# Attention followed by a GRU: an order of its own for the last batch of the attention

## The chip, the cores and the metric

The kernel runs on one core of a Trainium2 chip. The core has five engines that work side by side[...]: TensorE (PE in the profile; PEld is its weight load), VectorE (DVE), ScalarE (ACT), GpSimd (POOL) and SyncE (SP), which here issues DMAs. The metric is the device time of one execution in microseconds (us), as a median of several runs.

## The reference

The computation has two parts, each added to its input. `x` is (16, 256, 512): 16 batches of 256 time steps.

```python
# part 1: attention with 16 heads of 32 columns
scale, shift = split(cond @ W_emb + b_emb)
xn = rms_norm(x, g_norm) * (1 + scale) + shift
q, k, v = split(xn @ W_qkv)                # per head
q, k = rms_norm(q, g_q), rms_norm(k, g_k)
attn = softmax(q @ k.T * 32 ** -0.5)
o = attn @ v
x = x + o + o @ W_out
# part 2: a GRU over the 256 steps of the new x, started from cond
gi, gh = x_t @ W_ih + b_ih, h @ W_hh + b_hh
r, z = sigmoid(i_r + h_r), sigmoid(i_z + h_z)
n = tanh(i_n + r * h_n)
h = (1 - z) * n + z * h
out = x + hs
```

All arithmetic is in float32.

## The kernel before

The attention runs batch by batch, and in a batch by `NG` = 4 groups of `HG` = 4 heads. One group of one batch is a slot. `manual_schedule` makes the order in which the Python code issues instructions the order of each engine's queue (PE, DVE, ACT and POOL); semaphores are put in by the framework from the tiles that instructions read and write, so an instruction waits when it reaches the head of its queue, and all that is queued behind it waits too.

The work of a group, by function:

- `logits(b, g)` (L315): PE multiplies q and k of four heads into the PSUM banks lg0 to lg3, one bank a head.
- `maxima` (L332): DVE takes the negated row maxima, `neg`. `exps` (L340): ACT forms the exponentials, two instructions a head, into `attn`, with the row sums in `den`.
- `normalize` (L348, L351): DVE forms the reciprocals `rden`, POOL (or DVE) multiplies `attn` by them.
- `turn` (L224): PE transposes the four normalised heads, 32 small transposes into four banks. A bank holds one half of the rows of two heads. `put_turned` (L378) copies the four banks to `attnT` in SBUF, a string such as "vvva" naming the engine for each (v is DVE, a is ACT).
- `weigh` (L388): PE multiplies `attnT` with `v` into one bank. `put_weighed` (L399): ACT copies it to `oT`, which holds the attention's result, transposed, for all batches.

The slots are staggered: while the logits, maxima and exponentials of one group `w` are formed, the group before, `prev`, is transposed, copied and weighed. In batches 0 to 14 the slots (`slot0` to `slot3`) also hold the projections of the next batch, so PE has other work. Batch 15 has no next batch; its slots are `slot_last`:

```python
turn(prev, "AXYZ"); maxima(w, range(HG)); exps(w, range(HG))
put_turned(prev, "vvva")
normalize(w)            # in the last group heads 2 and 3 on DVE
weigh(prev, "A"); put_weighed(prev)
```

The main loop calls `logits(b, g)` ahead of it, and after the loop the last group is turned, copied ("vava") and weighed.

`attnT` has one buffer. PSUM has eight banks; in the attention they are the tags lg0 to lg3 (pool `ps_lg`) and A, X, Y, Z (pool `ps`). `work.close()` gives all of these back, and the GRU part opens three pools of its own: `ps_g` for the three gates (r, z, n), `ps_i` and `ps_o` with two buffers each for the input and output projections.

The GRU part works in stretches of `TI` = 16 time steps. `output_step` (L652, tile o) multiplies `wo` with `oT` (128 matmuls for a stretch, in four chunks m of 32), `put_output` (L685) adds each chunk to `xT`, the transposed x (DVE transposes it from `xin`, L667), and `input_step` (L652, tile gi) multiplies `wih` with `xT` (384 matmuls for a stretch). For the first stretch both run ahead of the recurrence; for the others they fill PE between the steps, four products a step (`FILL`). A step's own work is `state_part` (L714), the transposes L726 and the gates' arithmetic. `store_last` stores the last steps' results through a PSUM bank.

Of the kernel before, what the change touches and what calls it, by code (L numbers as in the profile page):

```python
# [19 lines left out]
def kernel(  # L20
# [57 lines left out]
    p1 = work.enter_context(tc.tile_pool(name="p1", bufs=1))  # L78
    p2 = work.enter_context(tc.tile_pool(name="p2", bufs=2))
    small = work.enter_context(tc.tile_pool(name="small", bufs=4))  # L80
    ps_lg = work.enter_context(tc.tile_pool(name="ps_lg", bufs=1, space=PSUM))
    ps = work.enter_context(tc.tile_pool(name="ps", bufs=1, space=PSUM))

# [136 lines left out]
    def turn_block(dst, src):  # L220

        for r in range(R):
            q = slice(QR * r, QR * r + QR)
            nc.tensor.transpose(dst[r], src[q], ident[q, q])  # L224
# [80 lines left out]
    def logits(b, g):  # L305

        w = Group()
        w.b, w.g = b, g
        w.lg = [
            ps_lg.tile([P, NT, T], F32, tag=f"lg{i}", name=f"lg_{b}_{g}_{i}") for i in range(HG)  # L310
        ]
        for n in range(NT):
            for i in range(HG):
                r = slice(i * DH, (i + 1) * DH)
                nc.tensor.matmul(  # L315
                    w.lg[i][:, n, :],
                    qT[r, g, n * P : (n + 1) * P],
                    kT[r, g, :],
                    start=True,
                    stop=True,  # L320
                )
        w.neg = small.tile([P, HG, NT], F32, tag="neg", name=f"neg_{b}_{g}")
# [23 lines left out]
    def normalize(w, heads=range(HG), engine=nc.gpsimd):  # L346
        r = slice(heads[0], heads[-1] + 1)
        nc.vector.reciprocal(w.rden[:, r, :], w.den[:, r, :])  # L348
        for i in heads:
            for n in range(NT):  # L350
# [2 lines left out]
                    ALU.mult, ALU.mult,  # L353
                )

    def turn(w, banks=("lg0", "lg1", "lg2", "lg3")):


        if w is None:
            return  # L360
        w.tp = [tile_ps(f"tpa_{w.b}_{w.g}_{i}", banks[i], (P, R, NT, NT, QR)) for i in range(HG)]
        for i in range(HG):
            for n in range(NT):
                for k in range(NT):
                    turn_block(
                        [w.tp[i // R * R + r][:, i % R, k, n, :] for r in range(R)],
                        w.attn[i][:, n, k * P : (k + 1) * P],
                    )
        w.attnT = p1.tile([P, HG, NT, T], F32, tag="attnT", name=f"attnT_{w.b}_{w.g}")

    def put_turned(w, engines):

        if w is None:
            return
        for i, e in enumerate(engines):
            h, r = i // R * R, i % R
            dst = w.attnT[:, h : h + R].rearrange("p h k (n r c) -> p h k n r c", n=NT, r=R)[:, :, :, :, r]
            (nc.scalar.copy if e == "a" else nc.vector.tensor_copy)(dst, w.tp[i])  # L378

    def weigh(w, bank):  # L380
        if w is None:
# [11 lines left out]
                    stop=(k == NT - 1),  # L393
                )

    def put_weighed(w):
        if w is None:
            return
        nc.scalar.copy(oT[:, w.g, :, w.b], w.o)  # L399

    class Stats:

# [108 lines left out]
            put_v(m, 1, st.v1)  # L511
        put_weighed(prev)

    def slot_last(g, w, prev):

        turn(prev, "AXYZ")
        maxima(w, range(HG))
        exps(w, range(HG))
        put_turned(prev, "vvva")
        if g < NG - 1:  # L520
            normalize(w)
        else:
            normalize(w, (0, 1))
            normalize(w, (2, 3), nc.vector)
        weigh(prev, "A")
        put_weighed(prev)

    E = mybir.EngineType
    ORDERED = {E.PE, E.DVE, E.Activation, E.Pool}
    with tc.manual_schedule(engines=ORDERED):  # L530

        nc.scalar.preload_act_table_set("natural_log_exp_and_others")
        st = Batch()
        norm_first(0)
        batches[0].rs.first()
        norm_apply(0, batches[0].rs.second())
        load_x(2)
# [42 lines left out]
        for b in range(B):  # L580
            for g in range(NG):
                w = logits(b, g)
                if b + 1 < B:
                    (slot0, slot1, slot2, slot3)[g](b, w, prev, st)
                else:
                    slot_last(g, w, prev)
                prev = w
        turn(prev)
        put_turned(prev, "vava")
        weigh(prev, "X")  # L590
        put_weighed(prev)

# [25 lines left out]


    gru = ctx.enter_context(tc.tile_pool(name="gru", bufs=2))
    ps_g = ctx.enter_context(tc.tile_pool(name="ps_g", bufs=1, space=PSUM))
    ps_i = ctx.enter_context(tc.tile_pool(name="ps_i", bufs=2, space=PSUM))
    ps_o = ctx.enter_context(tc.tile_pool(name="ps_o", bufs=2, space=PSUM))


    bhn_rows = gru.tile([P, P], F32, name="bhn_rows", bufs=1)
# [4 lines left out]


    gates = []
    for name in ("r", "z", "n"):
        gt = ps_g.tile([P, P], F32, tag=f"g{name}", name=f"g{name}")
        nc.vector.memset(gt, 0.0)
        gates.append(gt)

    TI = 16
    NI = T // TI
    NM = 3 * KC
    FILL = (KC + NM) * KC // TI
# [221 lines left out]
```

## Time and profile before

| | |
|---|---|
| Median of 3 runs | 1809.34 us (1808.86 to 1810.82) |
| The profiled execution | 1810.63 us, its span 1808.8 us |
| Granted TensorE clock, mean of the span | 0.994 |
| PE busy in the span | 1736.3 us (96%) |
| DVE, ACT and POOL busy | 1131.9, 819.8 and 314.4 us |
| Last batch, first logits to the first input projection | 610.18 to 656.86 us |
| First input projection | 656.86 to 677.8 us |
| Recurrence, 256 steps | 677.6 to 1808 us |

Busy time of PE is modelled, as matmuls are pipelined: a busy PE is not PE at its peak. The span is cut into stages by the times at which PE's groups of instructions start. In a timeline a row is a start, a duration, the engine, the line and the operation with its output and inputs, then how many instructions were merged into it and, in brackets, the idle time of the engine just before it and who ended it. In a table of stages a row has the stretch and its length, then the busy time of each engine with its number of instructions, the granted clock of PE (1.00 is full speed), the share of the DMA engines and GB/s. The chain of waits lists, in order of time, the work that the end of the program was waiting for.

### The profile page before, as it was taken

How to read it: one execution, taken by the hardware profiler on the slowest of the kernel's cores; microseconds unless marked ns; L12 is line 12 of the kernel's file. 1: busy time of each engine (PE TensorE's matmuls, PEld its weight loads, DVE VectorE, ACT ScalarE, POOL GpSimd, SP SyncE). 2: the span in 40 equal slices, each digit the busy share in tenths (PEclk: the TensorE clock that was granted, in tenths of full speed). 3: DMA queues.
4: the chain of work that ended last, by engine and by line, in shares of the span. 5: the costliest groups of instructions: out<-in, count | busy, mean ns of one | idle time of the engine just before them, and what ended most of it. 6: DMA issues, size and time to landing. Idle time of an engine off the chain costs nothing.

```text
span 1808.8 us, 92032 instructions
## 1 busy us (share of the span) xinstructions
PE 1736.3 (96%) x40754; PEld 1192.8 (66%) x40754; DVE 1131.9 (63%) x3762; ACT 819.8 (45%) x2764; POOL 314.4 (17%) x769
## 2 busy tenths in 40 slices
PE   6999999999999799999999999999999999999975
PEld 2444444444444458878887887888888788878865
DVE  3777777777776625656666566566566566665555
ACT  3777777777777633333332333333323333333322
POOL 0344433444334410000000000000000000000000
PEclk9999999999999889999999999999999999999999
DMA  7200000000000110011011101101110100000000
GB/s 263 54 14 14 14 26 13 14 14 14 14 2 2 71 25 10 16 22 21 16 18 21 18 16 21 21 16 19 22 18 16 21 16 10 13 13 10 10 15 15
DMA packets 146222, 43.73 MB, mean 24 GB/s; under 512 B 137899, under 2 KB 138031, under 8 KB 145823
## 3 DMA queue, kind: packets, MB, share of 16 engines
q1 hardware_dynamic: 145287, 36.72, 8.8%
q8 instruction: 320, 5.24, 1.2%
q10 hardware_dynamic: 536, 1.12, 0.2%
q14 instruction: 79, 0.65, 0.1%
HBM read 29.41 MB, written 8.39 MB: 21 GB/s over the span
## 4 chain that ended last, share of the span: by engine, by line
PE 84%; ACT 8%; DVE 5%; issue 2%; DMA 1%; POOL 0%; ACTq 0%; DVEq 0%
PE gi L652 17%; PE gr L714 13%; PE qkv L250 13%; PE gn L714 12%; PE gz L714 11%; ACT attn L340 6%; PE o L652 6%; PE lg L315 4%; PE o L388 4%; PE tpa L224 3%; DVE neg L332 1%; DVE tr L726 1%; PE tpqk L224 1%; PE tpx L224 1%; ACT z L798 0%
## 5 line engine op out<-in xcount | busy, mean ns | idle before, releaser
L652 PE MATMUL gi<-xT,wih 128*32 128x256 f32 x6144 | 364.7, 379 | 0.0
L250 PE MATMUL qkv<-wq,xnT 128*32 128x512 f32 x3072 | 356.4, 598 | 0.5 <-DVE xnT L242 0.5
L351 POOL TENSOR_SCALAR attn<-attn,rden 128x256 f32<-128x256 f32 x508 | 232.4, 479 | 411.3 <-DVE rden L348 278.7
L714 PE MATMUL gr<-whh,h 128*16 128x128 f32 x8160 | 272.1, 274 | 25.2 <-DVE h L818 24.1
L340 ACT ACTIVATE attn<-lg,neg 128x256 f32<-128x256 f32 x512 | 234.3, 483 | 89.0 <-DVE neg L332 52.3
L714 PEld LDWEIGHTS gr<-whh,h 128*16 128x16 f32 x8160 | 200.5, 96 | 108.7 <-DVE h L818 108.7
L714 PE MATMUL gn<-whh,h 128*16 128x128 f32 x8160 | 269.5, 273 | 0.0
L714 PE MATMUL gz<-whh,h 128*16 128x128 f32 x8160 | 269.4, 273 | 0.0
L820 POOL TENSOR_TENSOR y<-xT,h 128x64 f32<-128x64 f32 x255 | 81.4, 319 | 1072.7 <-DVE h L818 1035.3
L652 PEld LDWEIGHTS gi<-xT,wih 128*32 128x32 f32 x6144 | 196.1, 110 | 100.9
L789 ACT ACTIVATE r<-r 128x64 f32<-128x64 f32 x256 | 65.6, 256 | 380.5 <-DVE r L788 380.5
L726 DVE STREAM_TRANSPOSE tr<-gr 128x128 f32<-128x128 f32 x256 | 81.1, 317 | 237.2 <-PE gr L714 237.2
L714 PEld LDWEIGHTS gn<-whh,h 128*16 128x16 f32 x8160 | 224.8, 97 | 0.0
L714 PEld LDWEIGHTS gz<-whh,h 128*16 128x16 f32 x8160 | 224.7, 97 | 0.0
L250 PEld LDWEIGHTS qkv<-wq,xnT 128*32 128x32 f32 x3072 | 88.5, 110 | 181.0 <-issue 166.9
L332 DVE TENSOR_REDUCE neg<-lg 128x2 f32<-128x512 f32 (+1 forms) x320 | 163.1, 576 | 70.0 <-PE lg L315 69.6
L696 ACT ACTIVATE gi<-gi,cols 128x256 f32<-128x256 f32 x192 | 91.0, 474 | 165.0 <-PE gi L652 165.0
L726 DVE STREAM_TRANSPOSE tr<-gn 128x128 f32<-128x128 f32 x256 | 81.1, 317 | 76.0 <-PE gn L714 76.0
L652 PE MATMUL o<-oT,wo 128*32 128x256 f32 x2048 | 121.7, 379 | 0.7 <-ACT oT L399 0.7
L795 ACT ACTIVATE n<-n 128x64 f32<-128x64 f32 x256 | 65.6, 256 | 99.3 <-DVE n L794 98.7
L340 ACT ACTIVATION_READ_ACCUMULATOR attn<-lg,neg 128x1 f32 x512 | 110.3, 215 | 0.0
L224 PEld LDWEIGHTS tpa<-ident,attn 64*128 64x128 f32 x2048 | 77.1, 142 | 40.3 <-issue 26.3
(99 smaller groups left out, 1743.0 us busy)
## 6 DMA issues: line engine op xcount, KB each, us to landing
x<-in_x_dram SPq DMA_DIRECT2D x16, 512.0 KB, 3.2
xin<-in_x_dram SPq DMA_DIRECT2D x256, 32.0 KB, 2.8
out_dram<-osb SPq DMA_DIRECT2D x248, 32.0 KB, 2.3
wq<-in_L_cond_W_qkv_dram SPq DMA_DIRECT2D x12, 256.0 KB, 4.3
wih<-in_L_cond_W_ih_dram SPq DMA_DIRECT2D x4, 768.0 KB, 11.9
whh<-in_L_cond_W_hh_dram SPq DMA_DIRECT2D x4, 768.0 KB, 5.9
we<-in_L_cond_W_emb_dram SPq DMA_DIRECT2D x2, 512.0 KB
we<-in_L_cond_W_emb_dram ACTq DMA_DIRECT2D x2, 512.0 KB, 7.2
```

What stands on the lines that cost most here:

```text
L224: nc.tensor.transpose(dst[r], src[q], ident[q, q])
L250: nc.tensor.matmul(a[32 * j : 32 * j + 32, :], batches[b].xnT[:, k, n * P + 32 * j : n * P + 32 * j + 32], wq[:, k, s * D : (s + 1) * D], ...
L315: nc.tensor.matmul(w.lg[i][:, n, :], qT[r, g, n * P : (n + 1) * P], kT[r, g, :], start=True, stop=True,)
L332: nc.vector.tensor_reduce(w.neg[:, i, n], w.lg[i][:, n, :], AX.X, ALU.max, negate=True)
L340: nc.scalar.activation(a[:, n, :], w.lg[i][:, n, :], AF.Exp, bias=w.neg[:, i, n : n + 1], accum_out=w.den[:, i, n : n + 1],)
L351: engine.tensor_scalar(w.attn[i][:, n, :], w.attn[i][:, n, :], w.rden[:, i, n : n + 1], 1.0, ALU.mult, ALU.mult,)
L388: nc.tensor.matmul(w.o[i * DH : (i + 1) * DH, :], v[:, k, h * DH : (h + 1) * DH], w.attnT[:, i, k, :], start=(k == 0), stop=(k == NT - 1),)
L652: nc.tensor.matmul(acc[32 * j : 32 * j + 32, :], w[:, k, m * P + 32 * j : m * P + 32 * j + 32], rhs, start=(k == 0), stop=(k == KC - 1),)
L696: nc.scalar.activation(gis[grp][:, m].rearrange("p t b -> p (t b)"), acc["i"], AF.Identity, bias=bcols[:, m : m + 1],)
L714: nc.tensor.matmul(gates[g][32 * j : 32 * j + B, :], hT[:, k, :], whh[:, k, g * D : (g + 1) * D].rearrange("p (q j c) -> p j q c", q=KC, c ...
L726: nc.vector.transpose(tr.rearrange("p q b -> p (q b)"), gates[g])
L820: (nc.gpsimd if t + 1 < T else nc.vector).tensor_tensor(y[:, :, tl * B : (tl + 1) * B], xTs[grp][:, :, ti, :], h, ALU.add)
```

## The change

Four things change together. Batch 15 leaves the main loop (`range(B - 1)`) and `slot_last` is replaced by `last_batch`, which orders the four groups anew; the weighted sum of a group is issued one slot later, after the next logits. `turn` is split into `turn_pair` (two heads, two banks) and `put_turned` into `put_turned_bank`, and `put_weighed` takes an engine. The output projection of the first 16 steps, formerly at the start of the GRU part, is `project_first(k)`: it goes by k, the four groups of `oT`, into two banks that hold two chunks each, and it is issued inside `last_batch`; two additions of 512 columns take the place of four of 256. And the PSUM pools of the attention stay open for the whole kernel: the tiles of the GRU part are given banks of it by name.

```diff
-    ps_lg = work.enter_context(tc.tile_pool(name="ps_lg", bufs=1, space=PSUM))
-    ps = work.enter_context(tc.tile_pool(name="ps", bufs=1, space=PSUM))
+    ps_lg = ctx.enter_context(tc.tile_pool(name="ps_lg", bufs=1, space=PSUM))
+    ps = ctx.enter_context(tc.tile_pool(name="ps", bufs=1, space=PSUM))
...
+    def turn_pair(w, pair, banks):
+        if pair == 0:
+            w.attnT = p1.tile([P, HG, NT, T], F32, tag="attnT", name=f"attnT_{w.b}_{w.g}")
+        tps = [tile_ps(f"tpa_{w.b}_{w.g}_{pair}_{r}", banks[r], (P, R, NT, NT, QR)) for r in range(R)]
...
+    def put_turned_bank(w, i, engine):
...
-    def put_weighed(w):
+    def put_weighed(w, engine=nc.scalar):
...
+    def project_first(k):
+        if k == 0:
+            first.extend(tile_ps(f"first_{i}", f"lg{i}", (P, 2, TI * B)) for i in range(KC // 2))
+        for m in range(KC):
+            for j in range(4):
+                nc.tensor.matmul(
+                    first[m // 2][32 * j : 32 * j + 32, m % 2, :],
+                    wo[:, k, m * P + 32 * j : m * P + 32 * j + 32],
+                    oT[:, k, 0:TI, :].rearrange("p t b -> p (t b)"),
+                    start=(k == 0 and m % 2 == 0),
+                    stop=(k == KC - 1),
+                    skip_group_check=True,
+                )
+
+    def last_batch(prev):
+        b, before = B - 1, None
+        w = logits(b, 0)
+        for g in range(NG):
+            if before:
+                weigh(before, "Z")
+            turn_pair(prev, 0, "AX")
+            maxima(w, (0, 1))
+            exps(w, (0, 1))
+            if before:
+                put_weighed(before, nc.vector)
+            turn_pair(prev, 1, "YZ")
+            maxima(w, (2, 3))
+            exps(w, (2, 3))
+            put_turned_bank(prev, 0, nc.vector)
+            normalize(w, (0, 1))
+            put_turned_bank(prev, 2, nc.vector)
+            put_turned_bank(prev, 1, nc.scalar)
+            put_turned_bank(prev, 3, nc.scalar)
+            if g < NG - 1:
+                normalize(w, (2, 3))
+                before, prev, w = prev, w, logits(b, g + 1)
+        project_first(0)
+        project_first(1)
+        normalize(w, (2,), nc.vector)
+        normalize(w, (3,))
+        turn_pair(w, 0, ("lg2", "lg3"))
+        turn_pair(w, 1, "AX")
+        weigh(prev, "Z")
+        put_turned(w, "vava")
+        put_weighed(prev)
+        weigh(w, "Y")
+        put_weighed(w, nc.vector)
+        project_first(2)
+        project_first(3)
...
-    for name in ("r", "z", "n"):
-        gt = ps_g.tile([P, P], F32, tag=f"g{name}", name=f"g{name}")
+    for name, bank in (("r", "A"), ("z", "X"), ("n", "Y")):
+        gt = tile_ps(f"g{name}", bank, (P, P))
...
-            acc["o"] = ps_o.tile([P, TI * B], F32, tag="o", name=f"o_{grp}_{m}")
+            acc["o"] = tile_ps(f"o_{grp}_{m}", ("lg0", "lg1")[m % 2], (P, TI * B))
...
-            acc["i"] = ps_i.tile([P, TI * B], F32, tag="gi", name=f"gi_{grp}_{m}")
+            acc["i"] = tile_ps(f"gi_{grp}_{m}", ("Z", "lg2")[m % 2], (P, TI * B))
...
-        tp = ps_o.tile([P, KC, P], F32, tag="o", name=f"tpy_{tl}")
+        tp = tile_ps(f"tpy_{tl}", ("lg1", "lg0")[n == 1], (P, KC, P))
...
-        for i in range(KC * KC):
-            output_step(0, i)
-            if i % KC == KC - 1:
-                put_output(0, i // KC)
+        for i, o in enumerate(first):
+            a = xTs[0][:, 2 * i : 2 * i + 2].rearrange("p q t b -> p q (t b)")
+            nc.vector.tensor_tensor(a, o, a, ALU.add)
```

More of the change, by code (lines that the diff above doesn't have):

```diff
@@ L321, in logits @@
                 )
+        w.turned = []
         w.neg = small.tile([P, HG, NT], F32, tag="neg", name=f"neg_{b}_{g}")
@@ L354, in normalize @@
                 )
+    def turn_pair(w, pair, banks):
+        if pair == 0:
+            w.attnT = p1.tile([P, HG, NT, T], F32, tag="attnT", name=f"attnT_{w.b}_{w.g}")
+        tps = [tile_ps(f"tpa_{w.b}_{w.g}_{pair}_{r}", banks[r], (P, R, NT, NT, QR)) for r in range(R)]
+        for i in range(R):
+            for n in range(NT):
+                for k in range(NT):
+                    turn_block(
+                        [tp[:, i, k, n, :] for tp in tps],
+                        w.attn[R * pair + i][:, n, k * P : (k + 1) * P],
+                    )
+        w.turned += tps
     def turn(w, banks=("lg0", "lg1", "lg2", "lg3")):
@@ L360, in turn @@
             return
[L361 to L369, printed above, removed]
+        for pair in range(HG // R):
+            turn_pair(w, pair, banks[R * pair : R * pair + R])
+    def put_turned_bank(w, i, engine):
+        h, r = i // R * R, i % R
+        dst = w.attnT[:, h : h + R].rearrange("p h k (n r c) -> p h k n r c", n=NT, r=R)[:, :, :, :, r]
+        (nc.scalar.copy if engine is nc.scalar else nc.vector.tensor_copy)(dst, w.turned[i])
     def put_turned(w, engines):
@@ L375, in put_turned @@
         for i, e in enumerate(engines):
-            h, r = i // R * R, i % R
-            dst = w.attnT[:, h : h + R].rearrange("p h k (n r c) -> p h k n r c", n=NT, r=R)[:, :, :, :, r]
-            (nc.scalar.copy if e == "a" else nc.vector.tensor_copy)(dst, w.tp[i])
+            put_turned_bank(w, i, nc.scalar if e == "a" else nc.vector)
     def weigh(w, bank):
@@ L394, in weigh @@
                 )
-    def put_weighed(w):
+    def put_weighed(w, engine=nc.scalar):
         if w is None:
             return
-        nc.scalar.copy(oT[:, w.g, :, w.b], w.o)
+        (nc.scalar.copy if engine is nc.scalar else nc.vector.tensor_copy)(oT[:, w.g, :, w.b], w.o)
     class Stats:
@@ L512, in slot3 @@
         put_weighed(prev)
[L514 to L522, printed above, removed]
-            normalize(w, (0, 1))
-            normalize(w, (2, 3), nc.vector)
-        weigh(prev, "A")
-        put_weighed(prev)
+    TI = 16
+    first = []
+    def project_first(k):
[10 more added lines that the diff above has]
+                    skip_group_check=True,
+                )
+    def last_batch(prev):
[13 more added lines that the diff above has]
+            put_turned_bank(prev, 0, nc.vector)
+            normalize(w, (0, 1))
+            put_turned_bank(prev, 2, nc.vector)
[12 more added lines that the diff above has]
+        put_turned(w, "vava")
+        put_weighed(prev)
+        weigh(w, "Y")
+        put_weighed(w, nc.vector)
+        project_first(2)
+        project_first(3)
+    E = mybir.EngineType
     E = mybir.EngineType
@@ L579 @@
         prev = None
-        for b in range(B):
+        for b in range(B - 1):
             for g in range(NG):
                 w = logits(b, g)
[L583 to L586, printed above, removed]
+                (slot0, slot1, slot2, slot3)[g](b, w, prev, st)
                 prev = w
[L588 to L591, printed above, removed]
+        last_batch(prev)
     TG = P // B
@@ L622 @@
     gru = ctx.enter_context(tc.tile_pool(name="gru", bufs=2))
-    ps_g = ctx.enter_context(tc.tile_pool(name="ps_g", bufs=1, space=PSUM))
-    ps_i = ctx.enter_context(tc.tile_pool(name="ps_i", bufs=2, space=PSUM))
-    ps_o = ctx.enter_context(tc.tile_pool(name="ps_o", bufs=2, space=PSUM))
     bhn_rows = gru.tile([P, P], F32, name="bhn_rows", bufs=1)
@@ L635 @@
     gates = []
-    for name in ("r", "z", "n"):
-        gt = ps_g.tile([P, P], F32, tag=f"g{name}", name=f"g{name}")
+    for name, bank in (("r", "A"), ("z", "X"), ("n", "Y")):
+        gt = tile_ps(f"g{name}", bank, (P, P))
         nc.vector.memset(gt, 0.0)
         gates.append(gt)
-    TI = 16
     NI = T // TI
```

## The prediction

> **What bounds the kernel now.** I read the page's slices first (section 2). PE is at 90% or more nearly everywhere, and the two slices with a lower granted clock lie at about 590 to 680 us, so whatever the last batch loses is lost there. Then the table of stages, one row for each slot of the last batch, from one logits start to the next (the last row is the last slot with everything up to the first input projection):
>
> ```profile
> core 0: us, PE busy (x) PEld busy (x) DVE busy (x) ACT busy (x) POOL busy (x), PEclk, DMA share, GB/s
> 610.18:619.17 8.99, 5.75 (x76) 3.34 (x76) 4.55 (x9) 5.42 (x19) 4.87 (x12) 0.85 0.89 349
> 619.17:628.05 8.88, 5.91 (x68) 3.04 (x68) 4.54 (x9) 4.82 (x18) 3.64 (x9) 0.69 0.01 3
> 628.05:637.20 9.15, 6.22 (x68) 3.39 (x68) 4.55 (x9) 4.81 (x18) 3.69 (x9) 0.69 0.01 2
> ```
>
> The reader is to see that a slot lasts 9.0 us and no engine is busy in more than about two thirds of it: the slot is a chain, not a full engine. PE's timeline says which:
>
> ```profile
> 627.24 2.09 PE L315 MATMUL lg<-kT,qT 32*128 32x256 f32 x16
> 629.26 1.55 PE L224 MATMUL tpa<-ident,attn 64*128 64x64 f32 x32
> 633.14 0.76 PE L388 MATMUL o<-attnT,v 128*32 128x256 f32 x4 [2.34 <-DVE attnT L378]
> 634.50 1.92 PE L388 MATMUL o<-attnT,v 128*32 128x256 f32 x12 [0.59 <-ACT attnT L378]
> 636.35 2.09 PE L315 MATMUL lg<-kT,qT 32*128 32x256 f32 x16
> ```
>
> The chain of waits over the same stretch agrees:
>
> ```profile
> 632.38 1.58 ACT attn L340 x7
> 633.97 0.48 ACT attnT L378
> 634.50 1.92 PE o L388 x12
> 636.42 2.02 PE lg L315 x16
> ```
>
> So a slot is logits (2.0), first maxima (0.9), eight exponentials (3.75, from 630.22 to 633.97), ACT's copy of the last turned bank (0.53 with its wait), weighted sum (1.92), and only then the next logits: 9.1 us. The next logits need none of the last two; they are merely behind them in PE's order.
>
> After the last exponential of all (643.08), the tail runs to the first input projection:
>
> ```profile
> 649.93 7.11 PE L652 MATMUL o<-oT,wo 128*32 128x256 f32 x128 [0.68 <-ACT oT L399]
> 656.86 20.90 PE L652 MATMUL gi<-xT,wih 128*32 128x256 f32 x384
> ```
>
> That is 13.78 us, 7.11 of them output projection that could not start before the last oT. Last, stretches of 3.41 us, because PE's matmuls come in two speeds here:
>
> ```profile
> 613.03:616.44 3.41, 0.62 (x4) 0.14 (x4) 2.86 (x6) 3.41 (x15) 0.07 (x1) 1.00 1.02 410
> 616.44:619.85 3.41, 3.35 (x28) 1.79 (x28) 0.00 (x0) 0.60 (x2) 3.41 (x8) 0.50 0.60 249
> 619.85:623.26 3.41, 1.50 (x40) 1.07 (x32) 3.02 (x6) 2.15 (x9) 0.17 (x1) 1.00 0.00 2
> 623.26:626.68 3.42, 2.36 (x16) 0.76 (x16) 1.52 (x4) 2.07 (x9) 1.42 (x4) 0.50 0.00 0
> 626.68:630.09 3.41, 3.41 (x36) 2.06 (x34) 0.74 (x3) 0.60 (x1) 2.23 (x5) 0.50 0.02 5
> 630.09:633.50 3.41, 1.07 (x26) 0.72 (x22) 3.41 (x7) 3.28 (x15) 0.00 (x0) 1.00 0.00 0
> ```
>
> A stretch with PE busy 0.62, 1.50 or 1.07 us is followed by one at clock 0.50; a full one is followed by 1.00; one with 2.36 at half clock stays at half. At 0.50 logits take 2.0 us instead of 1.15 (the 610.18 one), a weighted sum 1.92 instead of 1.05.
>
> [...] the first maximum starts at 611.35, only when the logits end (611.33), though its half was written earlier: a consumer here waits for the whole bank. [...]
>
> **Part 1, weighted sums one slot later.** New PE order: logits, sum of the group before, transposes, next logits. I count from E, the end of a slot's exponentials. The next logits can start only there for head 3 (its bank), and the three heads that were free earlier do not help much, as the second half of every head is queued after it. At full clock:
> - Logits E+0.05 to E+1.15. Maxima of heads 0 and 1 from 1.17 to 2.43 (0.67 for head 0, 0.60 for each other). Exponentials start 0.87 after the first maximum, as at 629.35 and 630.22: 2.04 to 5.79. So the period is 5.8.
> - Beside this: ACT copies banks 1 and 3 in 0 to 1.17 (two took 1.14 at 606.60), while it would wait for maxima anyway. The weighted sum runs 1.2 to 2.25. DVE now evacuates it between the maxima. That copy is not in the trace; a DVE read of 128x256 from PSUM took 0.42 (L685) to 0.48 (L299), ACT's strided one 0.60, so 0.42 to 0.60, and I take 0.45: 2.45 to 2.9. Behind that copy stand the maxima of heads 2 and 3, ready at 3.5 and 4.1; ACT wants head 2 at 3.85, so the copy is hidden with 0.3 to spare.
> - Transposes 2.25 to 3.65 (1.38 for 32). They need POOL's normalisation: heads 2 and 3 of the group before, started after ACT's last read, end at 2.15. Bank Z is free at 2.9. DVE then copies bank 0 (0.68), reciprocal (0.17; two of 4 columns in place of one of 8, +0.15), bank 2. ACT sums to 3.75 + 1.17 = 4.9, DVE to 4.6, PE to 3.6 in 5.8.
>
> At half clock: logits to 2.05, sum to 3.97, its copy to 4.45; head 2's maximum comes at 5.1, and the exponentials, ready for it at 4.75, slip by 0.4. The period is 7.05.
>
> Which clock? Slot 0 is as before (E0 = 615.97). Between its transposes (end 612.6) and 616.44 PE now has the first logits of four heads, about 0.43 us each, so some 1.8 us of 3.41, between the 1.50 that lowered the clock and the 2.48 that kept it (647.16 to 650.57). I take "lowered" there, the next window full of work raises it, and later windows hold about 2.6 us. Three periods: 6.5 + 6.5 + 5.8 = 18.8, so E3 = 634.8 against 643.08. **8.3 us gained** (5.9 if half throughout, 9.7 if full).
>
> **Part 2, the tail.** From E3, at full clock: the projection of k = 0 and 1 (2 x 32 matmuls at 1.73, from 7.11/128 less its start) begins at E3-2.15, when the transposes are done and lg0 and lg1 are read, and ends at E3+1.35. It fills PE's wait. Normalisation of head 2 on DVE (0.9) and head 3 on POOL (0.91) ends at E3+1.9. Transposes 1.35 to 2.75, sum of group 2 to 3.8. The copies of the last turned banks overwrite attnT, which this sum reads: new wait, 3.85 to 5.1 on both engines. Behind it on ACT is oT's copy of group 2 (to 5.6), for which only k = 2 waits. Last sum 4.5 to 6.15, DVE copy to 6.65; k = 2 from 6.15 to 7.85, k = 3 to 9.6. DVE's memsets, copies and two xT transposes (2.0 in all) lie beside these. Two additions of 512 columns replace four of 256 (0.42 each); the nearest is L276 with 0.65; the first ends at about 9.65, the second at 10.3, before k = 2 of the input projection. So gi starts at E3+9.7 against 13.78: **4.1 gained**, 1.6 if the clock stays at half.
>
> **Part 3, banks named.** The gates get A, X, Y, the two alternating pairs lg0/lg1 and Z/lg2: as many buffers with the same alternation as before. Cost nothing: 4 products per step and the same waits. It moves no DMA; SP's and POOL's queues keep their order in the recurrence. In the first 15 batches transposes come in the same order; cost nothing.
>
> **Sum.** 8.3 + 4.1 = 12.4. Span 1808.8 - 12.4 = 1796.4. The profiled execution took 1810.63, 1.8 around its span, so 1798.2; the median of the runs is 1.3 below it, so **1797.0**.
>
> **Rivals.** (B) The clock stays at half through the last batch: gains 5.9 and 1.6, 1801.8. For it: 2.83 us of 3.42 at half did not raise it (633.50 to 636.92). Against: PE's gaps shrink from 2.5 us to under 1. (C) The loop gains nothing, since DVE's copy of the sum between the maxima links PE's lateness to ACT: the exponentials would have to wait over 3 us in a slot, where my half-clock sum gives 0.4. Only the tail is left, 1805.2. (D) Slower: the recurrence pays for the new banks. Its 256 steps take some 4.34 us each with PE busy 199.8 of 200 us, so an added wait on a bank in the fill lengthens each step. From 12.4/240 = 52 ns in each step with fill it eats the gain; at 100 ns the time is 1821. Against it: the same number of buffers.
>
> **How the numbers follow.** My forecast, 1795.5 (all full clock) to 1799.5, has 0.64; B 0.18; C 0.07; D 0.11. The range 1795.0 to 1802.0 holds the first two and leaves out C and D. About 0.2% (3.6 us) is what can be told from no change: C lies at that edge and is split, so faster 0.85, same 0.04, slower 0.11.
>
> **What would show it.** Right: logits to logits 5.8 to 6.5 us; a weighted sum directly after logits; 64 output matmuls before the last transposes; gi at about 644.5; 1130.4 us from the recurrence's start to the end unchanged. Wrong: exponentials of head 2 waiting long on maxima (C), clock 0.50 in most windows (B), a recurrence longer than 1130.4 (D).

## The result, and the profile after

The changed kernel takes 1796.77 us (median of 5 runs, 1796.44 to 1803.15) where the kernel before takes 1810.37 (5 runs, 1808.86 to 1812.19). The ratio is 0.9932, with a 95% interval of 0.9914 to 0.995. The profiled execution took 1796.65 us, its span 1794.8. The run of 1803.15 had a mean granted clock of 0.992 where the other four had 0.995 to 0.998; there is no profile of it, so why it was lower stays open.

The span is 14.0 us shorter. Cut at the same points in both traces, it falls into these pieces (us):

| | before | after | difference |
|---|---|---|---|
| start to the first logits of batch 15 | 610.18 | 611.32 | +1.14 |
| these logits to the first slot's last exponential | 5.79 | 5.79 | 0 |
| from last exponential to last exponential, three slots | 8.89, 9.11, 9.11 | 6.55, 5.43, 5.43 | -9.70 |
| tail, to the first input projection | 13.78 | 9.93 | -3.85 |
| first input projection | 20.94 | 20.96 | +0.02 |
| recurrence and end | 1131.04 | 1129.44 | -1.60 |

In the profiles of this study that leave the first 15 batches as they are, the first piece lies between 610.0 and 611.9 us, so its +1.14 is within what one execution differs from another. The three pieces that got shorter are the result.

The table of stages for the changed kernel, one row for each of the last three slots and one for the tail (columns as in the one for before):

```profile
617.16:623.71 6.55, 6.11 (x64) 3.31 (x64) 4.49 (x11) 4.83 (x19) 3.02 (x8) 0.74 0.37 150
623.71:629.14 5.43, 4.96 (x64) 3.00 (x65) 4.51 (x11) 4.72 (x19) 3.67 (x9) 1.00 0.01 3
629.14:634.53 5.39, 5.36 (x94) 3.50 (x98) 4.60 (x12) 4.68 (x19) 3.62 (x9) 1.00 0.02 5
634.53:644.45 9.92, 8.95 (x165) 5.45 (x153) 5.40 (x14) 2.52 (x5) 2.10 (x5) 1.00 0.04 7
```

DVE and ACT do in 5.43 us what took 9.1; only the first row has half clock in it (0.74 as a mean). PE's timeline for one slot shows the new order:

```profile
623.71 1.13 PE L315 MATMUL lg<-kT,qT 32*128 32x256 f32 x10 [0.22 <-ACT attn L341]
624.77 1.07 PE L398 MATMUL o<-attnT,v 128*32 128x256 f32 x16
625.77 1.52 PE L224 MATMUL tpa<-ident,attn 64*128 64x64 f32 x32
627.22 0.80 PE L315 MATMUL lg<-kT,qT 32*128 32x256 f32 x4
628.23 0.69 PE L315 MATMUL lg<-kT,qT 32*128 32x256 f32 x2 [0.22 <-DVE attnT L381]
629.14 1.13 PE L315 MATMUL lg<-kT,qT 32*128 32x256 f32 x10 [0.22 <-ACT attn L341]
```

The weighted sum (o) now follows the logits without a wait, and the logits wait only for ACT's last exponential (ACT attn, the release at 629.14). Between them the first halves of the logits of three heads come in one by one, as their banks come free. DVE's timeline over the same stretch:

```profile
624.46 1.35 DVE L333 TENSOR_REDUCE neg<-lg 128x1 f32<-128x256 f32 x3 [0.59 <-PE lg L315]
625.90 0.61 DVE L409 COPY oT<-o 128x256 f32<-128x256 f32 x1
626.37 1.25 DVE L333 TENSOR_REDUCE neg<-lg 128x2 f32<-128x512 f32 x2
```

The first maximum starts at 624.46, 0.75 us after the logits resumed and 0.38 before the last of them ends (623.71 + 1.13). The copy of the sum stands between the maxima, as written. PE's tail:

```profile
632.63 3.66 PE L533 MATMUL first<-oT,wo 128*32 128x256 f32 x64
636.22 1.22 PE L224 MATMUL tpa<-ident,attn 64*128 64x64 f32 x32
637.37 1.07 PE L398 MATMUL o<-attnT,v 128*32 128x256 f32 x16
639.42 1.44 PE L398 MATMUL o<-attnT,v 128*32 128x256 f32 x14 [0.97 <-DVE attnT L381]
...
640.70 3.83 PE L533 MATMUL first<-oT,wo 128*32 128x256 f32 x62
644.45 5.82 PE L696 MATMUL gi<-xT,wih 128*32 128x256 f32 x104
```

Half of the output projection is done before the last transposes, and the one wait left on PE is 0.97 us for copies into attnT. Last, stretches of 3.41 us, counted from the one at half clock (617.88 to 621.29):

```profile
614.47:617.88 3.41, 2.76 (x15) 1.51 (x16) 1.99 (x5) 3.41 (x14) 2.08 (x5) 1.00 1.02 420
617.88:621.29 3.41, 3.41 (x36) 1.53 (x37) 2.14 (x5) 2.13 (x9) 1.58 (x4) 0.50 0.50 201
621.29:624.71 3.42, 2.98 (x36) 1.79 (x33) 2.60 (x7) 2.90 (x10) 1.73 (x4) 1.00 0.00 0
624.71:628.12 3.41, 3.27 (x53) 2.02 (x52) 3.32 (x7) 2.79 (x13) 1.92 (x5) 1.00 0.02 5
```

One stretch of half clock is left, after the first slot; before, six of nine stretches from 616.44 to 647.16 were at half, in pieces of 3.41 or 6.83 us that began at 616.44, 623.26, 633.50 and 643.74.

### The profile page after: what moved, and what is told of

It reads as the page before. It is cut to its first block, busy times and chain, and to the rows that moved or that the text cites. A ratio compares the mean times of both kernels' runs of the same rounds, so it can differ in the third digit from the quotient of the medians.

```text
span 1794.8 us, 92039 instructions
## 1 busy us (share of the span) xinstructions
PE 1732.5 (97%) x40754; PEld 1191.5 (66%) x40754; DVE 1130.5 (63%) x3762; ACT 820.2 (46%) x2764; POOL 315.7 (18%) x771
## 3 DMA queue, kind: packets, MB, share of 16 engines
q10 hardware_dynamic: 536, 1.12, 0.2%
HBM read 29.41 MB, written 8.39 MB: 21 GB/s over the span
## 4 chain that ended last, share of the span: by engine, by line
PE 85%; ACT 8%; DVE 4%; issue 2%; DMA 1%; POOL 0%; ACTq 0%; DVEq 0%
PE gi L696 18%; PE gr L758 13%; PE qkv L250 13%; PE gn L758 13%; PE gz L758 11%; ACT attn L341 6%; PE o L696 5%; PE lg L315 4%; PE o L398 3%; PE tpa L224 3%; DVE neg L333 1%; DVE tr L770 1%; PE tpqk L224 1%; PE tpx L224 1%; ACT v L270 0%
## 5 line engine op out<-in xcount | busy, mean ns | idle before, releaser
L696 PE MATMUL o<-oT,wo 128*32 128x256 f32 x1920 | 114.6, 379 | 0.0
L753 ACT COPY gn<-bhn_rows 128x128 f32<-128x128 f32 x256 | 68.9, 269 | 75.3 <-DVE tr L770 75.3
```

Source lines behind the costliest of these rows:

```text
L696: nc.tensor.matmul(acc[32 * j : 32 * j + 32, :], w[:, k, m * P + 32 * j : m * P + 32 * j + 32], rhs, start=(k == 0), stop=(k == KC - 1),)
L753: nc.scalar.copy(gates[2], bhn_rows)
```

## The experiments

The times of runs that were not made together differ by a microsecond or two (the kernel before has medians from 1809.52 to 1811.37 in its five sets of runs), which is about what the experiments are to tell apart. So I read the stages of the last batch from each trace and give the time beside them. "Periods" are the three times from last exponential to last exponential, "last batch" is from its first logits to the first input projection (46.68 before, 33.13 after).

### Order and clock apart

**e9_fill_before** asks what the old order costs at full clock:

```diff
+    def fill(n):
+        t = tile_ps("fill", "lg0")
+        for _ in range(n):
+            for j in range(4):
+                nc.tensor.matmul(
+                    t[32 * j : 32 * j + 32, :], ident[:, 32 * j : 32 * j + 32], wo[:, 0, :],
+                    start=True, stop=True,
+                )
...
+        fill(2)
         weigh(prev, "A")
```

> The kernel before with the same 1.8 us of matmuls that compute nothing needed in each of its last four slots, ahead of the weighted sum, where PE waits; nothing else is changed. Theory (of the 9.7 us that the loop gained, the order alone is worth 5.6 us and the rest is the clock): at full clock a slot is logits 1.1 + maximum 0.87 + exponentials 3.75 + copy 0.53 + sum 1.05 = 7.3 us instead of 9.0, so about 5 us less than the kernel before with more work. Rival (the clock follows from the order and is not to be had by work alone, or the filler holds up the sum): 9 us a slot, time as before or above.

Measured: periods 7.30, 7.30, 7.30, last batch 40.20, time 1805.05 (ratio to before 0.9973, 0.9961 to 0.9985). PE's timeline, with L519 as the filler:

```profile
617.85 1.15 PE L315 MATMUL lg<-kT,qT 32*128 32x256 f32 x16
618.92 1.85 PE L224 MATMUL tpa<-ident,attn 64*128 64x64 f32 x32
620.96 1.92 PE L519 MATMUL fill<-wo,ident 128*32 128x512 f32 x16 [0.18 <-ACT attn L340]
622.81 0.63 PE L388 MATMUL o<-attnT,v 128*32 128x256 f32 x4
624.16 1.06 PE L388 MATMUL o<-attnT,v 128*32 128x256 f32 x12 [0.73 <-ACT attnT L378]
625.15 1.15 PE L315 MATMUL lg<-kT,qT 32*128 32x256 f32 x16
```

The old order is untouched, the wait for ACT's copy too (0.73), and yet a slot is 1.7 us shorter: logits last 1.15 instead of 2.09, the sum 1.06 instead of 1.92. Work that nobody needs made the kernel 5 us faster: the mean granted clock of the profiled execution was 1.0, where before it was 0.994.

**e5_fill** does the same to the changed kernel, once, in its first slot (`if g == 0: fill(2)` ahead of the next logits).

> The changed kernel with 1.8 us of matmuls that compute nothing needed (16 of 512 columns, in lg0, which the next logits overwrite), ahead of the second group's logits, in the wait of PE in the first slot. Theory (the 6.55 us of the second slot are half clock, set by the sparse stretch ahead of it): clock 1.00 through the last batch, periods 5.43, 5.43, 5.43, so 1.1 us less than the changed kernel although PE does more. Rival (the second slot is long because the loads of whh take the DMA engines, or because of the order at the start): its period stays at 6.5 or grows.

Measured: periods 5.43, 5.42, 5.43, last batch 32.01, time 1795.70 (ratio 0.9921, 0.9905 to 0.9938; by the time alone it is not apart from the changed kernel). No stretch of the last batch is at half clock (the mean of the profiled execution is 0.999). PE's timeline, with L548 as the filler:

```profile
613.68 1.92 PE L548 MATMUL fill<-wo,ident 128*32 128x512 f32 x16 [0.65 <-ACT attn L341]
615.70 1.84 PE L315 MATMUL lg<-kT,qT 32*128 32x256 f32 x16
617.47 1.07 PE L398 MATMUL o<-attnT,v 128*32 128x256 f32 x16
618.48 1.50 PE L224 MATMUL tpa<-ident,attn 64*128 64x64 f32 x32
```

The sum takes 1.07 us here where the changed kernel's second slot has 1.94. The rival, that loads of whh make that slot long, falls: they are still there, with a DMA share of 0.48 in this slot (616.36 to 621.79) against 0.37 in the changed kernel's.

With these two, the loop's gain can be divided. At full clock three old slots take 21.9 us and three new ones 16.3: the order is worth 5.6. Half clock added 27.1 - 21.9 = 5.2 to the old and 17.4 - 16.3 = 1.1 to the new ones: the other 4.1 of the 9.7 are clock. The 5.6 stand on two kernels at full clock throughout. The 4.1 are those of two executions, and another could have other ones: in e1_banks, below, three old slots took 25.65 us, which is 3.75 of half clock and not 5.2.

### The weighted sum put back

**e4_sum_first** undoes one line of the new order:

```diff
-            if before:
-                weigh(before, "Z")
             turn_pair(prev, 0, "AX")
...
+                weigh(prev, "Z")
                 before, prev, w = prev, w, logits(b, g + 1)
```

> The changed kernel with only the weighted sum put back in front of the next logits; split transposes, DVE's evacuation and the early projection stay. Theory (logits stood behind a sum that waits for ACT's copies): period copies 1.15 + sum 1.05 + logits 1.1 + maximum 0.87 + exponentials 3.75 = 7.9 us at full clock, up to 8.9 with half clock, so 23.7 to 26.7 us over three slots instead of 17.4; time 1803 to 1806. Rival (the gain is from the split pairs, the evacuation by DVE and the copies after the exponentials): periods stay under 6.2 us, time within 2 us of the changed kernel.

Measured: periods 9.61, 9.42, 9.61, time 1806.42 (ratio 0.9978, 0.997 to 0.9987). PE's timeline:

```profile
626.38 1.94 PE L398 MATMUL o<-attnT,v 128*32 128x256 f32 x16 [2.56 <-ACT attnT L381]
628.24 1.89 PE L315 MATMUL lg<-kT,qT 32*128 32x256 f32 x16
```

PE stands 2.56 us before the sum, for ACT's copies after the exponentials, and the logits stand behind it. All the rest of the change was there, and the slot was longer than in the kernel before, as two copies of ACT now stand ahead of the sum and not one (1.02 us from the last exponential to the sum, 0.53 before). So the loop's gain is not to be had without the new place of the sum. Whether it is to be had by that alone, with the old transposes and copies, was not tried. The periods went above my 8.9; the clock was at half in 20.5 of the 28.6 us (mean 0.52 and 0.68 in the first two slots).

### One part alone

**e1_banks** is the kernel before with only the open pools and the named banks.

> The kernel before with one part of the change alone: the PSUM pools stay open and the GRU part's tiles are given banks by name; last batch and output projection in the old order. Theory (banks cost nothing): same time as before within 0.2%, last batch from first logits to first input projection 46.7 us as before, recurrence 1130.4 us within 1 us. Rival (the banks carry part of the result, since the recurrence of the changed kernel took 1128.8 in its profile): recurrence about 1129 us and 1.5 us less in all.

Measured: 1808.78 (ratio 0.999, 0.9984 to 0.9997). The recurrence and the end took 1130.68; from the first to the last step, by the starts of the transposes of gate r, it was 1120.18 (before 1120.91, after 1119.30). The last batch took 43.51 with periods 8.79, 8.17, 8.69, although not one instruction of it is other than before: the stretches of half clock begin at other places (618.4 instead of 616.4 us, and four of 3.4 us before 646 us in place of six). So a comparison of two last batches from one profile each has some 3 us of luck in it. The banks alone are not the result. Of the 1.8 us by which this median is lower, the recurrence has 0.7 in the profile, which belongs to the positions treated under e12_shift; the rest I can't assign.

**e2_order** has the new order and the projection back in the GRU part (`output_step` for the first stretch, as before).

> The changed kernel with the first output projection back in the GRU part, in front of the input projection. Theory (loop and tail gain separately): slots from last exponential to last exponential as in the changed kernel (6.55, 5.43, 5.43 us), tail back to some 13.8 us, so 3.9 us above the changed kernel, about 1800.7. Rival (the projection inside the tail only fills a wait that the new order opened by itself): tail about 10 us also without it, time within 1 us of the changed kernel.

Measured: 1801.07 (ratio 0.9948, 0.9932 to 0.9965), 4.3 above the changed kernel. Periods 6.07, 5.43, 7.20 and a tail of 12.68, together 31.4 against 27.3. The sum is as expected, its parts are not: half clock covered the last of the three periods (628.3 to 635.2), and 16 of the 128 output matmuls went ahead of the last transposes, which made the tail shorter than 13.8.

**e3_project** has the early projection in the old order:

```diff
+        if g == NG - 1:
+            project_first(0)
+            project_first(1)
         weigh(prev, "A")
```

> The kernel before with named banks and the first output projection begun early (k = 0 and 1 ahead of the weighted sum of the last slot, k = 2 and 3 after the last weighted sum), all else in the old order. Theory: the 3.5 us of k = 0 and 1 go into PE's waits of the last slot; first logits to input projection 42.4 us instead of 46.7, about 1806. Rival (the old order has no wait left for it, since the weighted sum is pushed back by as much): gain under 1 us.

Measured: 1803.44 (ratio 0.9961, 0.9947 to 0.9976), periods 8.39, 9.11, 8.81, tail 8.59, last batch 40.68. The waits took the work: 5.2 us less in the tail than before. It also kept the clock up there (the sum at 643.86 took 1.05 us; before, 643.74 to 647.16 was at half clock), which my 4.3 had left out. The two parts do not add: by the medians they are 9.5 and 7.2 us below before, and the changed kernel, which has both, is 13.6 below. In the last batch they are 9.5 and 6.0 against 13.6, and e3_project has 2.0 more from a shorter recurrence (e12_shift). The 2 us by which the last batch's parts exceed the whole are no more than its luck of 3 us, so whether both win back the same half clock is not shown.

### Where the slot's bound is now

**e8_act_fill** puts the copy of the sum back on ACT, in the kernel of e5_fill.

> The kernel of e5_fill (full clock throughout, periods 5.43) with the evacuation of the weighted sum back on ACT, between its exponentials of heads 1 and 2. Theory (ACT is on the path that sets the slot, DVE is not): ACT's copy of 0.60 us, some 0.45 to 0.6 of it added, makes the periods 5.9 to 6.0, 1.5 us more than e5_fill. Rival (the copy hides on ACT as well as on DVE): 5.43.

Measured: periods 5.81, 5.82, 5.81, tail 10.78, time 1795.46. ACT's timeline:

```profile
618.82 0.48 ACT L341 ACTIVATE attn<-lg,neg 128x256 f32<-128x256 f32 x1
...
619.27 0.60 ACT L409 COPY oT<-o 128x256 f32<-128x256 f32 x1
619.64 0.50 ACT L341 ACTIVATE attn<-lg,neg 128x256 f32<-128x256 f32 x1
```

The copy adds 0.38 to each slot, for the next exponential starts before it has ended. ACT is on the path that sets the slot, and on DVE the same copy costs nothing at full clock. The second pair of transposes also waits for it (1.25 us on PE), so the tail is longer. By the time it can't be told from e5_fill; in the profile its recurrence is 1.1 us shorter (more on that under e12_shift).

Its clock was not full throughout, which the expectation had taken for granted, and that shows one thing more. The table of stages has half clock in the second slot:

```profile
615.79:621.60 5.81, 4.39 (x68) 2.78 (x64) 4.10 (x9) 5.10 (x20) 4.05 (x10) 1.00 0.43 172
621.60:627.42 5.82, 5.60 (x64) 3.35 (x64) 4.11 (x9) 5.11 (x21) 2.72 (x7) 0.71 0.01 3
```

The sum took 1.94 us there, and yet the slot was no longer. In the changed kernel the same slow sum cost 1.12 us, as DVE's and ACT's timelines have it:

```profile
620.50 0.60 DVE L409 COPY oT<-o 128x256 f32<-128x256 f32 x1 [1.24 <-PE o L398]
620.95 1.26 DVE L333 TENSOR_REDUCE neg<-lg 128x2 f32<-128x512 f32 x2
...
621.73 0.47 ACT L341 ACTIVATE attn<-lg,neg 128x256 f32<-128x256 f32 x1 [1.01 <-DVE neg L333]
```

DVE stood before the copy for the slow sum, the maxima of heads 2 and 3 stood behind the copy, and ACT waited for them. So a slow PE reached ACT through the place of DVE's copy. The next run agrees: there the copy stands behind these maxima, and a slot of 4.72 us had half clock in it too (618.4 to 621.9), against 4.73 at full clock in e10_pairs_fill.

**e6_pairs** gives the groups 1 to 3 logits in pairs of heads, and puts DVE's copy of the sum behind the maxima of heads 2 and 3.

> The changed kernel with the logits of the groups 1 to 3 of the last batch in pairs of heads (heads 0 and 1 whole, then 2 and 3) and DVE's evacuation of the sum behind the maxima of heads 2 and 3. Theory (at full clock the period is logits after the last exponential, first maximum, exponentials; the first pair no longer waits for the last exponential): ACT is the bound, copies 1.12 + exponentials 3.75 = 4.9 us a slot, about 1.6 us less than the changed kernel over three slots. Rival (POOL's normalisation or DVE takes its place): periods stay at 5.4 or more.

Measured: periods 4.72, 5.78, 4.90, tail 11.68, time 1796.16. The path was right, the place of the copy was not. PE's timeline in the second of these slots:

```profile
623.84 0.77 PE L224 MATMUL tpa<-ident,attn 64*128 64x64 f32 x17
625.96 0.71 PE L224 MATMUL tpa<-ident,attn 64*128 64x64 f32 x15 [1.35 <-DVE oT L411]
626.60 2.06 PE L317 MATMUL lg<-kT,qT 32*128 32x256 f32 x16
```

The second pair of transposes wants bank Z, from which the copy reads, and stood for it 1.35 us. The logits behind it ran late, and half clock followed from 628.7 on.

**e10_pairs_fill** puts the copy between the maxima of heads 2 and 3 and adds the filler; **e11_pairs_v** takes needed work as the filler, half of the last projection of v (the lines with `project`):

```diff
-        project(m, 1, 2, (2, 3) if last else (2,), st.v1)
+        if not last:
+            project(m, 1, 2, (2,), st.v1)
...
+        order = [(n, i) for p in (0, 2) for n in range(NT) for i in (p, p + 1)]
...
+            maxima(w, (2,))
             if before:
                 put_weighed(before, nc.vector)
+            if g == 0:
+                project(b, 1, 2, (2, 3), st.v1)
...
+            maxima(w, (3,))
```

> The changed kernel with logits in pairs of heads, DVE's evacuation between the maxima of heads 2 and 3 (in e6_pairs it stood behind both, and the second pair of transposes waited 1.35 us for it), and the filler of e5_fill. Theory: full clock, ACT is the bound, periods 4.9, 4.9, 4.9 and a tail of 9.95, so 2.7 us less than the changed kernel in its profile, about 1794. Rival (the clock falls again in a later slot, as in e6_pairs): one period near 5.8, under 2 us gained.

> As e10_pairs_fill, but with needed work as the filler: the last two k of the last batch's projection of v (32 matmuls, 1.75 us) move from the end of batch 14, where PE has no wait, into the first slot of batch 15, between its two pairs of transposes, and DVE copies v there. Theory: the clock stays full without idle work and batch 15 starts 1.75 us earlier, so about 1.8 us less than e10_pairs_fill, about 1792. Rival (POOL's normalisation of the last group of batch 14, 3.65 us, now ends later than the transposes want it, and the slot gets longer by as much): equal to e10_pairs_fill.

Measured: e10_pairs_fill periods 5.12, 4.73, 4.73, tail 10.63, last batch 31.00, time 1795.05 (ratio 0.9915, 0.9901 to 0.9928). e11_pairs_v periods 5.46, 4.72, 4.73, tail 10.64, last batch 31.34, time 1794.21 (0.9913, 0.9899 to 0.9926). Two slots and the tail of e10_pairs_fill in the table of stages:

```profile
622.84:627.57 4.73, 4.61 (x64) 3.02 (x64) 4.40 (x10) 4.73 (x20) 3.37 (x9) 1.00 0.01 3
627.57:632.30 4.73, 4.65 (x78) 3.05 (x82) 4.46 (x11) 4.72 (x20) 3.68 (x9) 1.00 0.01 2
632.30:642.93 10.63, 9.66 (x176) 5.89 (x168) 5.46 (x14) 2.54 (x6) 2.24 (x5) 1.00 0.04 8
```

ACT is busy 4.73 of 4.73 us: it is the bound, and only less work on it would shorten the slot. Two slots came out below the 4.9 that I expected, the first above it. 0.7 us come back in the tail, where PE has the same work in a row whenever the exponentials end, so slots and tail together gained 2.1 us on the changed kernel and not 2.7. e11_pairs_v has the lowest median of all, 2.6 us under the changed kernel, but the intervals overlap. The 1.8 us expected of it over e10_pairs_fill are not shown. By the medians it is 0.84; in the two profiles the span is 1.8 shorter, but all of that is the start of batch 15 (609.82 against 611.93), which differs by as much between executions. In its last batch PE waited 0.91 us for DVE's copy of v and 0.45 for the sum's in the next slot.

**e7_tail** moves the sum of group 2 and its copy ahead of the last transposes, and k = 2 of the projection ahead of the last sum.

> The changed kernel with the tail in another order: the weighted sum of group 2 and its copy ahead of the last transposes, k = 2 of the projection between the transposes and the last sum. Theory (the last copies wait for attnT, which that sum reads, and PE waits 1.0 us for them): the wait goes, the tail takes 9.3 us instead of 9.93. Rival (the tail is PE's work from end to end, the wait only moves): 9.9 us.

Measured: 1798.59 (ratio 0.9935, 0.9921 to 0.995), tail 11.24, but with half clock from 629.0 to 635.9. From the end of the first 64 projection matmuls on, which is at full clock, it took 8.06 us (638.19 to 646.25) against 8.23 (636.22 to 644.45) in the changed kernel. PE's timeline:

```profile
642.06 1.05 PE L398 MATMUL o<-attnT,v 128*32 128x256 f32 x16
643.81 1.93 PE L533 MATMUL first<-oT,wo 128*32 128x256 f32 x32 [0.71 <-DVE bhn_wide L675]
646.25 4.09 PE L696 MATMUL gi<-xT,wih 128*32 128x256 f32 x72 [0.50 <-DVE xT L810]
```

The wait for attnT is gone, and two others stand in its place: 0.71 after the last sum and 0.50 for the additions to xT. What is left is 0.17 us where 0.6 were expected, so the rival was right.

### The 1.6 us of the recurrence

Its instructions are the same before and after. In the trace of before single DVE instructions start late at steps 64 apart. DVE's timeline at step 13, and one step on:

```profile
738.71 0.23 DVE L817 TENSOR_TENSOR h<-h,z 128x64 f32<-128x64 f32 x1 [0.46 <-ACT z L798]
...
743.09 0.23 DVE L817 TENSOR_TENSOR h<-h,z 128x64 f32<-128x64 f32 x1 [0.25 <-ACT z L798]
```

The wait is put down to ACT's z, but that had ended at 738.47 (738.21 + 0.26), so 0.21 us of the 0.46 are no wait for it. **e12_shift** adds only this to the kernel before:

```diff
         put_bhn()
+        pad = gru.tile([P, 1], F32, name="pad", bufs=1)
+        for _ in range(30):
+            nc.vector.memset(pad, 0.0)
```

> The kernel before with 30 one-column memsets more on DVE ahead of the recurrence, where DVE waits some 20 us for the input projection; nothing else is changed. In the profile of before, DVE starts single instructions 0.2 to 0.3 us late without a wait at steps 13, 77, 141, 205 and 41, 105, 169, 233 and 68, 132, 196 (64 apart), ACT at 30, 63, 96, 212; in the changed kernel only DVE's steps are others. Theory (the late starts follow the count of instructions on the engine, and the 1.6 us of the recurrence are such positions, not banks or arithmetic): DVE's steps move earlier by two or three, ACT's stay, and the recurrence from its first to its last step takes between 1119 and 1121.5 us, not the 1120.9 of before. Rival (they belong to transfers or to the banks): the same steps, 1120.9 as before.

Measured: from the first to the last step 1119.00 us, 1.9 less than before and 0.3 less than after. DVE's late steps are now 48, 112, 176 and 66, 130, 194 (again 64 apart), ACT's 30, 63, 96 and 212 are where they were. The time is 1809.56 (ratio 0.9992, 0.9983 to 1.0001), too uncertain to show 1.9 in 1809. DVE's steps did not simply move by the two or three that I expected.

The traces of all fourteen kernels, taken together, show where the late starts fall. Number the entries that a trace has for one engine from 0, those that only wait or signal included. In the recurrences 162 instructions of DVE and ACT start over 0.08 us later than the same operation usually does after what released it, or after the start of the instruction before it. Every one of the 162, and every late step of the kernel before that the expectation lists, has a number that leaves 63 when divided by 128 (1343 at step 13, 2239 at step 77). Between these two steps DVE has 896 entries, seven times 128, which is why late steps are 64 apart. Not every such place is late: in the trace of before DVE's entries 1215 (step 4) and 1855 (step 50) start within 0.01 us of the usual.

The kernels fall into groups by this count. Before, e2_order and e9_fill_before have 1159 entries of DVE ahead of the recurrence and take 1120.9 to 1121.0 us from the first to the last step, although e2_order has the named banks and the other two have not. The changed kernel and five more (e4_sum_first, e5_fill, e6_pairs, e7_tail, e10_pairs_fill) have 1157 and take 1119.3. ACT has 1879 entries ahead of it in all nine. So the 1.6 us go with this count and not with the banks: the change took two entries off DVE's list, and DVE's late starts fell on other steps. ACT's count has its share too: e1_banks and e11_pairs_v have 1158 on DVE, 1879 and 1878 on ACT, and take 1120.2 and 1119.3. The traces also have transfers of 8192 bytes of the kind "instruction" (83 in the trace of before). After 660 us one of them starts within 2 us of such a place, late start or not, at 602 of 602 places (43 of 43 in the trace of before); of 1205 entries with the remainders 0 and 32 it is so at 97. So the late starts stand where such a transfer starts. Whether the transfer is what holds the engine up was not tested.

## Why the prediction was right, and where it was off

It said 1797.0, in a range of 1795.0 to 1802.0, and 1796.8 was measured. The mechanism was right, and the sum was right to 0.2 us, but the second in part by luck: the parts of the change gained more than forecast, and the median of before that I started from was 1.0 below that of all five runs. That gi started at 644.45, as forecast, is luck too, for batch 15 began 1.14 us later.

- **What bounded the slot**: right. With only the sum back in front of the logits the slot is 9.6 us again (e4_sum_first), and the old order's full-clock chain comes to the 7.3 us that its links add up to (e9_fill_before).
- **Period at full clock**: 5.8 predicted, 5.43 measured. The term that failed is "the three heads that were free earlier do not help much". Only head 3's first half and the second halves are left after the last exponential, and head 0's bank is complete 0.75 us after the logits resume, not 1.12. Taken to its end in e10_pairs_fill, the same point gave 4.73.
- **Clock**: "lowered" for the second slot and 6.5 us was right (6.55). For the third I took 6.5, and it stayed at full clock with 5.43. The two together make the loop's gain 9.7 instead of 8.3. "Lowered" came true by luck. I put the sparse stretch at 1.8 us of PE work (0.43 for the logits of one head), and the profile has 2.76 there (0.69 for one head). By my own bounds, 1.50 that lowered the clock and 2.48 that kept it, 2.76 would have kept it. So PE's busy time was not the right measure: half clock followed 2.76, and the clock stayed full after 2.44 (638.36 to 641.77). The first of these stretches had logits of single heads, 32*128 in the timeline, the second sums and projections, 128*32. Whether that counts was not tried.
- **DVE's copy of the sum**: I took 0.45 in a range of 0.42 to 0.60; it is 0.60, with the next instruction 0.47 after its start, so the slot did not feel it at full clock. At half clock ACT waited 1.01 us for the maxima behind it (621.73) and not 0.4.
- **Tail**: 9.7 predicted, 9.93 measured. The new wait for attnT came where it was expected (0.97 us on PE), and e7_tail shows that it is not worth removing alone.
- **Banks, "cost nothing"**: no cost came (rival D), but Part 3 put the recurrence's change at nothing, and it fell by 1.6 us with the count of instructions alone.
- **Rivals**: B and C are out by the rows of stages: full clock in three of four, and maxima late for ACT in one slot only. The link that C named is real, though: it is the way by which half clock made that slot longer. The added +1.14 at the start was in no term.

In sum: 9.70 + 3.85 = 13.55 us where I had 12.4, then 1.60 - 1.14 on the two ends. The span fell by 14.0 where I had 12.4, and the median fell by 12.6 from the median before that I started from, 13.6 from that of all five.

## What to carry to other kernels

On an engine that takes its instructions in order, as PE does here (in e4_sum_first it stood 2.56 us before the sum, with the logits behind it), look for the instruction that waits and ask whether the one behind it needs its result; moving it one round later cost nothing here, since its inputs were by then long ready. Where TensorE waits as much as in the last batch before (0.62 to 1.50 us of work in the stretches of 3.41 us after which the clock fell to half), price each order at both clocks, and try filling a wait with work before reordering anything: even useless matmuls won 5 us here, and needed ones can be moved there (e11_pairs_v kept full clock with them). When the loop gets shorter, follow the new bound to the end (here ACT, at 4.73 of 4.73 us) and expect part of the gain back in the tail.

## What the runs showed of the hardware

- The same instructions took 46.68 and 43.51 us in the last batch of two kernels (before and e1_banks), as the stretches of half clock, six of 3.41 us in the one and four in the other, fell elsewhere. One filler of 1.9 us a slot made three slots 7.30 us each (e9_fill_before).
- PE busy 2.76 of 3.41 us was followed by half clock, 2.44 of 3.41 was not: PE's busy time as the profile models it does not decide it here.
- Single DVE and ACT instructions in a long unrolled stream start late without a wait, by 0.13 to 0.37 us in the traces of before and after. All 162 of them in fourteen traces stand at one place in each 128 entries of the engine's list, and an 8192-byte instruction transfer starts within 2 us of that place (602 of 602). With thirty more memsets on an idle DVE the recurrence took 1119.0 us instead of 1120.9 (e12_shift).
- What one stretch of half clock cost in the new order depended on what stood behind the slow sum: 1.12 us where DVE's copy of it stood ahead of the maxima that ACT wanted, 0.01 where ACT made the copy itself.
